# A graph-attention layer on one core: ScalarE fetches a tile in every 32nd pair, its rows between the copy and the exponentials, and SyncE stores before it loads

## The chip, the core and the metric

The kernel runs on one NeuronCore of a Trainium2 chip. Its engines work beside one another, each with its own queue of instructions: TensorE (PE, with its weight loads as PEld), VectorE (DVE), ScalarE (ACT), GpSimd (POOL) and SyncE (SP, which issues DMAs). Each engine takes its queue in order and waits at semaphores for the others. DMAs are issued from SP's, ACT's and POOL's queues. The metric is the time of one execution on the device in microseconds (us), the median over runs.

## The reference

The kernel computes one block of a graph network on 12,500 nodes of 128 features and 400,000 edges sorted by destination; self loops are added. Cut to what matters:

```python
h   = relu(layernorm(x))
hn  = ln(h, ln1_g, ln1_b)
x_l = hn @ W_l                 # for the source of an edge
x_r = hn @ W_r                 # for its destination
m     = leaky_relu(x_l[src] + x_r[dst] + edge_attr @ W_e, 0.2)   # 8 heads of 16
alpha = einsum('ehc,hc->eh', m, att)
a     = softmax of alpha over the edges of one destination, per head
g     = segment_sum(x_l[src] * a, dst) + bias
h2  = h + g
out = x + h2 + gelu(ln(h2, ln2_g, ln2_b) @ W1 + b1) @ W2 + b2
```

The self loops' edge attribute is the mean over all edges, so this mean has to be computed too. The sources of the edges are random, so `x_l[src]` is a gather of 400,000 rows of 528 bytes (128 features and 8 ones) from a table in device memory, `xl_dram`.

## The kernel before

**Start.** A first loop of 43 rounds normalises all nodes, computes `x_l` and stores it to `xl_dram` with four node tiles to a round. In the same rounds POOL gathers some raw rows of `x` (L339), DVE prepares the edge indices, and in round 14 the source indices are loaded: once as the table `src_sb` (128 edges down the partitions, one column to a tile), and once more, number by number, into `hand_sb`, one row of 128 indices for each tile that is fetched by hand (L840 to L847). In round 16 DVE multiplies these by the length of a row in bytes (L851).

**Edges.** 128 edges make a tile, four tiles a pair (of two units of 256 edges), and there are 782 pairs. The main loop (L1681) runs over rounds; in each round every stage works on another pair. In the order of their issue within a round, with the pair that a stage has in hand in round r:

- `gather` (r+4): four indirect gathers from POOL, one for each tile (L1078), into one of 12 row buffers `xs`.
- `own_heads` (r-7): DVE takes each head's own sums from `acc` into the record `rec` (L1215, L1221).
- `keep_turned` (r-5): ACT copies the turned weights from PSUM (L1197).
- `combine` (r): PE turns the gathered rows into `z` (L1143) and adds the destination's and edge's terms with a matmul (L1146).
- `apart` (r-2), `turn` (r-4), `collect` (r-6), `score` (r-2): PE's marking of foreign edges (L1152), transposition of the exponentials (L1192), weighted sums (L1206) and scores (L1167).
- `lowest` (r-3): DVE takes the lowest score (L1173). `slope` (r-1): ACT scales `z` (L1157). `bend` (r-1): DVE's leaky ReLU (L1162). `weigh` (r-3): ACT's two exponentials `p` (L1184). `place` (r+1): DVE marks destinations (L1129).

The order of the work is written out by hand in these tables; no planner moves it. Behind the stages of a round stand, in this order: the loads and sums for the mean edge attribute (`sum_load`, L1248, on SP's queue, every second round up to round 194), the steps of the node groups, the hand-fetched rows, a clearing of states every fourth round, the loads of the next windows every fourth round (`windows`, L1104 to L1119), and the store of one pair's record (`put`, L1230).

**Rows fetched by hand.** Some tiles are not gathered by POOL. In every 22nd pair from 30 on (35 pairs), SP fetches the last tile's 128 rows with one small DMA each; in every 64th pair from 77 on (11 pairs), ACT does. `hand` (L1037 to L1062) spreads the 128 rows over as many rounds as there are pairs in a step: about six rows to a round on SP, two on ACT. Before every 16 rows the queue reads 16 offsets from `hand_sb` into registers (L1010, seen as `TENSOR_LOAD`). The last row is issued seven rounds before its pair's round, and one round before it the queue waits until all rows have landed (L1043). Another 29 pairs read rows that were computed late (`late_dram`) and need no gather.

**Node groups.** Once all edges of some four node tiles are stored as states, a group's steps merge them with the self loop and run the rest of the layer (tables `steps`, and for the last two groups `soon`, `after` and `last_steps`, L1573 to L1657). A state load (`f_state`, L1292) waits for the stores of records. A store of a record waits for earlier accesses to the states unless it is declared free of them; that is done while SP still fetches rows (the list `fetched` is not empty). The second-last group has round 774, the last one 790.

Of the kernel before, what the change touches and what calls it, by code (L numbers as in the profile page):

```python
# [13 lines left out]
F32 = mybir.dt.float32  # L14
# [8 lines left out]
P = 128  # L23
# [52 lines left out]
BESIDE_EVERY = 64  # L76
BESIDE_FIRST = 77
BESIDE_LANDED = 3
BESIDE_AT = 64
BIG = 2.0**126  # L80
# [94 lines left out]
def tile_gnn(  # L175
# [112 lines left out]
    def load_consts():  # L288
        for i, v in enumerate((ln2_g, ln2_b, None, b1[0:P], b1[P : 2 * P])):
            if v is not None:  # L290
                nc.sync.dma_start(cols[:, 2 + i : 3 + i], column(v))
        nc.sync.dma_start(att_c, bass.AP(tensor=att.tensor, offset=att.offset, ap=[[1, C], [C, H], [1, 1]]))
        nc.sync.dma_start(we_sb, bass.AP(tensor=w_e.tensor, offset=w_e.offset, ap=[[P, DE], [0, QP], [1, P]]))
        nc.sync.dma_start(weh_sb[WN:P, :], w_e)
        nc.sync.dma_start(w1_sb, w1)
        nc.sync.dma_start(w2_sb, w2.rearrange("(k p) f -> p k f", p=P))
        nc.sync.dma_start(bias_r, row_bcast(bias, P))
        nc.sync.dma_start(b2_r, row_bcast(b2, P))
        nc.sync.dma_start(first_sb, bass.AP(tensor=dst.tensor, offset=dst.offset, ap=[[0, 1], [UP * U, NU // UP]]))
        for i in range(QP):  # L300
            nc.sync.dma_start(
                at_sb[:, BEHIND:, 1 + i],
                bass.AP(tensor=dst.tensor, offset=dst.offset + (UP * i + 1) * U, ap=[[0, 1], [QU * U, NQU]]),
            )

# [504 lines left out]
    with tc.manual_schedule():  # L810
# [15 lines left out]
        for r in range(max(max(len(qs), 9) + LAST + 1, 16 + PARTS, rows_at[-1] + KEPT + 1)):  # L826
# [11 lines left out]
            if r == 14:  # L838
                nc.sync.dma_start(src_sb, src)
                for at, h in ((0, hands), (BESIDE_AT, beside)):  # L840
                    nc.sync.dma_start(
                        hand_sb[at : at + len(h)],
                        bass.AP(
                            tensor=src.tensor, offset=src.offset + (h[0] + 1) * UP * KU - 1,
                            ap=[[h.step * UP * KU, len(h)], [NCH * K, P]],
                        ),
                    )  # L847
            if r == 16:
                for at, h in ((0, hands), (BESIDE_AT, beside)):
                    rows = hand_sb[at : at + len(h)]  # L850
                    nc.vector.tensor_scalar(rows, rows, float(XW * 4), None, op0=OP.mult)  # L851
# [101 lines left out]
def window_edges(  # L953
# [30 lines left out]
    with ExitStack() as es:  # L984
# [52 lines left out]
        def hand(r, w):  # L1037

            w["new"].clear()
            hands, n = w["pairs"], w["sems"]  # L1040
            i, k = divmod(r + HAND_LEAD + hands.step - hands[0], hands.step)
            if k == HAND_LEAD - 1 and 0 < i <= len(hands):
                all_here = w["queue"].wait_ge(w["landed"][(i - 1) % n], ((i - 1) // n + 1) * P * 16)  # L1043
                tc.declare_fence(all_here.ins, group=f"{w['name']}{i - 1}")
# [3 lines left out]
            if k == 0:  # L1048
                d["x"] = once.tile([P, XW], F32, name=f"{w['name']}{i % 2}")
            for e in range(P * k // hands.step, P * (k + 1) // hands.step):  # L1050
                if e % HAND_READ == 0:
                    d["at"] = words(
                        hand_sb[w["at"] + i : w["at"] + i + 1, e : min(e + HAND_READ, P)], (NT * P - 1) * XW * 4,
                        w["engine"],
                    )
                row = w["queue"].dma_start(
                    d["x"][e : e + 1, :].bitcast(U8), rows_at(xl_dram, d["at"][e % HAND_READ], 1, XW * 4)
                )
# [166 lines left out]
        def put(c):  # L1225
# [11 lines left out]
            if fetched:  # L1237
# [3 lines left out]
                )  # L1241

# [3 lines left out]
        def sum_load(i):  # L1246
            sums[i] = fin.tile([P, LW], F32, name="ea_s", tag="big", bufs=3)
            nc.sync.dma_start(  # L1248
# [295 lines left out]
        def f_put(d):  # L1544
# [4 lines left out]
            (LATE + 1, own_heads),  # L1549
            (5, keep_turned),  # L1550
# [6 lines left out]
            (1, slope),  # L1557
# [3 lines left out]
        )  # L1561
        late_stages = (
            (-WAHEAD, windows),
            (LATE + PUT, put),
# [115 lines left out]
        with tc.manual_schedule():  # L1680
            for r in range(-AHEAD, max(last_round, groups[-1]["round"] + 18)):  # L1681
                in_round(r, early, groups[:-2])
                for late, f in stages:
                    c = r - late
                    if 0 <= c < n_pr:
                        f(c)
                for late, f in sum_stages:
# [11 lines left out]
                for w in ways:  # L1699
                    hand(r, w)  # L1700
# [6 lines left out]
                for late, f in late_stages:  # L1707
                    c = r - late
                    if 0 <= c < n_pr:
                        f(c)  # L1710
# [354 lines left out]
```

## Time and profile before

| | |
|---|---|
| median of 3 runs | 3905.68 us (3905.53 to 3908.12) |
| profiled execution | 3904.92 us |
| its span, first to last instruction | 3903.2 us |
| busy: PE, PEld | 3414.5 us, 2329.9 us |
| busy: DVE, ACT, POOL | 2799.8 us, 2177.5 us, 2913.6 us |
| granted TensorE clock | 0.96 of full speed |

Times in the profile are in us from the span's start, unless marked ns. A row of a group of instructions names the line, the engine, the operation, what is written and read, and how often, and then its busy time, the mean of one in ns, and the idle time of the engine just before such instructions with what ended it. Issuing a DMA, reading registers and waiting at semaphores aren't counted as busy; rows marked SPq, ACTq and POOLq show such work on an engine's queue. A row of the waits gives who waited for whom, the total in us, how often, and the longest. A row of the timeline gives the start, the duration and, in square brackets, the idle time ahead of it. "Issue" in the chain or in the waits is time in which the engine waited for nothing that the profile shows. The name behind an arrow is inferred, and of several semaphores the last one is named.

### The profile page before, as it was taken

To read this page: it belongs to the slowest core of one execution; us is meant where nothing else is said; L and a number is where in the kernel's file an instruction comes from. 1 tells how busy PE (TensorE), PEld (TensorE's weight loads), DVE (VectorE), ACT (ScalarE), POOL (GpSimd) and SP (SyncE) were. 2 spreads that over 40 slices of the span, in tenths; PEclk is the share of its full clock that TensorE was granted. 3 is DMA by queue.
4 is the path that set the end of the run, shared out by engine and by line. 5 is a ranking of instruction groups with operands and counts; after the bars stand their busy time and mean duration, and the time that the engine had idled before them with its cause. 6 is when DMAs were issued, how large, how long until landed. Compare 5 with 4: busy or idle time off the path is not lost.

```text
span 3903.2 us, 70516 instructions
## 1 busy us (share of the span) xinstructions
PE 3414.5 (87%) x18461; PEld 2329.9 (60%) x18463; DVE 2799.8 (72%) x6142; ACT 2177.5 (56%) x4745; POOL 2913.6 (75%) x3092
## 2 busy tenths in 40 slices
PE   3588899889899989998999899999998989898988
PEld 3356566556566666665666666666666666666655
DVE  5577877777776776777777777777777767667665
ACT  6545555555565555555555555655555556456444
POOL 7777777777777777777777777777777777777773
PEclk6799999999999999999999999999999999999999
DMA  8767777777766666665565555555565555555553
GB/s 203 236 163 173 184 184 182 177 185 185 177 135 134 136 131 130 137 132 125 123 131 124 123 126 126 125 123 121 121 125 126 123 123 112 124 122 117 122 119 65
DMA packets 546765, 549.30 MB, mean 141 GB/s; under 512 B 248891, under 2 KB 425372, under 8 KB 545932
## 3 DMA queue, kind: packets, MB, share of 16 engines
q1 hardware_dynamic: 444290, 329.68, 34.3%
q0 software_dynamic: 98528, 214.12, 28.9%
q8 instruction: 150, 2.46, 0.3%
q14 instruction: 261, 2.14, 0.2%
q10 hardware_dynamic: 3536, 0.91, 0.1%
HBM read 482.08 MB, written 62.28 MB: 139 GB/s over the span
## 4 chain that ended last, share of the span: by engine, by line
PE 36%; POOL 24%; DMA 20%; issue 13%; DVE 2%; SPq 1%; ACT 0%; ACTq 0%; POOLq 0%
POOL xs L1078 24%; DMA xs<-xl_dram,src_sb 19%; PE z L1146 8%; PE acc L1206 8%; PE ab L1167 6%; PE pt_ps L1192 4%; PE z L1143 4%; PE ab L1152 2%; PE acc L1525 1%; DMA state<-rec 0%; DVE rec L1173 0%; PE acc L1500 0%; PE pt_ps L759 0%; DMA zw<-xr_dram 0%; PE acc L1328 0%
## 5 line engine op out<-in xcount | busy, mean ns | idle before, releaser
L1078 POOL DMA_INDIRECT xs<-xl_dram,src_sb x2963 | 2798.4, 944 | 904.3 <-issue 783.9
L1184 ACT ACTIVATE p<-ab,rec 128x256 f32<-128x256 f32 x1563 | 656.4, 471 | 923.6 <-DVE rec L1173 909.3
L1215 DVE TENSOR_TENSOR own<-acc,diag 128x272 f32<-128x272 f32 x782 | 342.6, 438 | 821.9 <-PE acc L1206 813.2
L1143 PE MATMUL z<-ident,xs 128*128 128x128 f32 x3079 | 564.7, 283 | 360.6 <-DMA xs<-xl_dram,src_sb 337.9
L1206 PE MATMUL acc<-xs,pt 128*128 128x136 f32 x6158 | 873.7, 286 | 0.0
L1143 PEld LDWEIGHTS z<-ident,xs 128*128 128x128 f32 x3079 | 395.3, 142 | 776.8 <-DMA xs<-xl_dram,src_sb 449.7
L1146 PE MATMUL z<-ea,zw 128*128 128x512 f32 x1564 | 828.0, 612 | 6.5 <-DMA xs<-xl_dram,src_sb 6.5
L1197 ACT COPY pt<-pt_ps 128x512 f32<-128x512 f32 x782 | 456.2, 583 | 643.6 <-PE pt_ps L1192 585.5
L1167 PE MATMUL ab<-m,negrep 128*128 128x512 f32 x1564 | 806.4, 597 | 0.2 <-issue 0.2
L1206 PEld LDWEIGHTS acc<-xs,pt 128*128 128x128 f32 x6158 | 800.7, 197 | 0.0
L1192 PEld LDWEIGHTS pt_ps<-ident,p 128*128 128x128 f32 x3125 | 408.0, 146 | 345.0 <-issue 269.7
L1162 DVE TENSOR_TENSOR m<-z,zs 128x512 f32<-128x512 f32 x782 | 533.6, 682 | 108.1 <-ACT zs L1157 106.2
L1129 DVE TENSOR_SCALAR ea<-dl,wid 96x516 f32<-96x516 bf16 x782 | 575.4, 736 | 8.0 <-DMA dl<-dc_dram 8.0
L1173 DVE TENSOR_REDUCE rec<-ab 128x2 f32<-128x512 f32 x781 | 539.0, 690 | 14.2 <-PE ab L1167 13.7
L1192 PE MATMUL pt_ps<-ident,p 128*128 128x128 f32 x3125 | 490.7, 281 | 0.6 <-ACT p L1184 0.6
L1157 ACT ACTIVATE zs<-z 128x512 f32<-128x512 f32 x782 | 471.8, 603 | 31.0 <-PE z L1146 31.0
L1221 DVE TENSOR_REDUCE rec<-own 128x34 f32<-128x272 f32 x782 | 340.9, 436 | 26.7
L1152 PE MATMUL ab<-ne,farw 128*128 128x512 bf16 (+1 forms) x781 | 306.8, 393 | 24.6 <-ACT p L1184 22.9
L1146 PEld LDWEIGHTS z<-ea,zw 128*128 128x128 f32 x1564 | 253.1, 202 | 7.3 <-issue 6.8
L1167 PEld LDWEIGHTS ab<-m,negrep 128*128 128x128 f32 x1564 | 245.8, 195 | 1.1 <-DMA ea_s<-in_ea_t 0.7
L1152 PEld LDWEIGHTS <-farw 128*128 128x128 bf16 x782 | 78.1, 100 | 211.9 <-issue 102.2
L1184 ACT ACT_TABLE_LOAD x102 | 130.9, 1283 | 1.8
(249 smaller groups left out, 2215.6 us busy)
## 6 DMA issues: line engine op xcount, KB each, us to landing
dl<-dc_dram SPq DMA_DIRECT2D x196, 396.0 KB
hand<-xl_dram SPq DMA_DIRECT2D x4480, 0.5 KB
ea<-in_ea_t SPq DMA_DIRECT2D x196, 256.0 KB
ea_s<-in_ea_t SPq DMA_DIRECT2D x98, 512.0 KB
xs<-xl_dram,src_sb POOLq DMA_INDIRECT x2963
beside<-xl_dram ACTq DMA_DIRECT2D x1408, 0.5 KB
state<-empty SPq DMA_DIRECT2D x98, 144.0 KB
f_st<-state SPq DMA_DIRECT2D x46, 288.0 KB
```

What stands on the lines that cost most here:

```text
L1078: nc.gpsimd.indirect_dma_start(out=xs[:, j, :], out_offset=None, in_=xl_dram, in_offset=bass.IndirectOffsetOnAxis(ap=src_sb[:, c * KP + j ...
L1129: nc.vector.tensor_scalar(d["ea"][0:WN].rearrange("p (a b) -> p a b", b=OW), d["dl"][0:WN].rearrange("p (a b) -> p a b", b=OS)[:, :, 0:OW] ...
L1143: nc.tensor.matmul(z[:, j * P : (j + 1) * P], row_of(c, j)[:, 0:P], ident, start=(j == 0), stop=False, is_transpose=True)
L1146: nc.tensor.matmul(z[:, :e], d["zw"], d["ea"][:, :e], start=False, stop=True)
L1152: nc.tensor.matmul(d["ab"][:, :e], d["far"], d["ne"][:, :e], start=True, stop=False)
L1157: nc.scalar.activation(d["zs"][:, :e], d["z"][:, :e], AF.Copy, scale=SLOPE)
L1162: nc.vector.tensor_tensor(d["m"][:, :e], d["z"][:, :e], d["zs"][:, :e], op=OP.max)
L1167: nc.tensor.matmul(d["ab"][:, :e], negrep.rearrange("p n h -> p (n h)"), d["m"][:, :e], start=False, stop=True)
L1173: nc.vector.tensor_reduce(d["rec"][:, :, CX], d["ab"].rearrange("p (u e) -> p u e", e=U), AX.X, OP.min)
L1184: nc.scalar.activation(d["p"][:, us], d["ab"][:, us], AF.Exp, bias=d["rec"][:, i, CX:SH], scale=-1.0)
L1192: nc.tensor.transpose(d["pt_ps"][:, js], d["p"][:, js], ident)
L1206: nc.tensor.matmul(d["acc"][:, i, :], d["pt"][:, j * P : (j + 1) * P], row_of(c, j), start=(j == js[0]), stop=(j == js[-1]),)
```

## The change

1. ACT fetches a tile in every 32nd pair from 45 on (23 pairs) and not in every 64th from 77 on (11). It issues four rows to a round, all between its copy (`keep_turned`) and its exponentials (`weigh`). `slope` goes ahead of the copy.
2. The hand-fetched indices aren't loaded a second time from device memory. In rounds 24 to 26 of the start, DVE copies their columns out of `src_sb` as floats, PE transposes them, and DVE multiplies and writes `hand_sb`.
3. SP issues the first half of a round's rows at the beginning of the round and the second half behind the node groups' steps; then come the store of a record, the loads of windows and the clearing, in this order. The loads for the mean edge attribute are issued by ACT. The registers of the next four stores are read behind a store.
4. The stores of the records of pairs 779 to 781 are declared free of other accesses to the states too, behind a wait for SP's last fetched rows.
5. The second-last node group's steps are drawn together: exponential, sums, output, statistics, root and scaling lie 1 to 5 rounds behind its state load, not 2 to 8.

```diff
-BESIDE_EVERY = 64
-BESIDE_FIRST = 77
+BESIDE_EVERY = 32
+BESIDE_FIRST = 45
+HAND_ROUND = 24
...
+    def hand_columns():
+        nc.vector.memset(hand_f, 0.0)
+        for at, h in ((0, hands), (BESIDE_AT, beside)):
+            first = (h[0] + 1) * UP * KU - 1
+            step = h.step * UP * KU
+            nc.vector.tensor_copy(
+                hand_f[:, at : at + len(h)], src_sb[:, first : first + step * (len(h) - 1) + 1 : step]
+            )
+    def hand_turn():
+        hand_ps["t"] = once_ps.tile([P, GN * P], F32, name="w_ps")
+        nc.tensor.transpose(hand_ps["t"][0 : BESIDE_AT + len(beside), 0:P], hand_f, ident)
+    def hand_bytes():
+        nc.vector.tensor_scalar(
+            hand_sb, hand_ps["t"][0 : BESIDE_AT + len(beside), 0:P], float(XW * 4), None, op0=OP.mult
+        )
...
-                for at, h in ((0, hands), (BESIDE_AT, beside)):
-                    nc.sync.dma_start(
-                        hand_sb[at : at + len(h)],
...
-        def hand(r, w):
+        def hand(r, w, share=(0, 1), behind=0):
...
-            for e in range(P * k // hands.step, P * (k + 1) // hands.step):
+            first, last = P * k // hands.step, P * (k + 1) // hands.step
+            for e in range(*(first + int((last - first) * x) for x in share)):
...
+            free = bool(fetched) or c > hands[-1]
+            if free and not fetched:
+                nc.sync.wait_ge(ways[0]["landed"][(len(hands) - 1) % LANDED], ((len(hands) - 1) // LANDED + 1) * P * 16)
             store = nc.sync.dma_start(states_at(d["put"])[:, 0:nu], d["rec"][0 : KN * H, 0:nu].bitcast(U8))
-            if fetched:
+            if free:
...
+            if c % QP == 0 and c + QP < n_pr:
+                ats(c // QP + BEHIND + 1)
...
-            nc.sync.dma_start(
+            nc.scalar.dma_start(
                 sums[i],
...
             (LATE + 1, own_heads),
+            (1, slope),
             (5, keep_turned),
...
-            (1, slope),
             (1, bend),
...
+        beside_at = {keep_turned: ()}
         late_stages = (
+            (LATE + PUT, put),
             (-WAHEAD, windows),
-            (LATE + PUT, put),
         )
...
-            (2, f_exp),
-            (3, f_den),
-            (4, f_out),
-            (5, f_h),
-            (6, f_stats),
-            (7, f_root),
-            (8, f_scale),
-            (8, f_rest),
+            (1, f_exp),
+            (2, f_den),
+            (2, f_out),
+            (3, f_h),
+            (3, f_stats),
+            (4, f_root),
+            (5, f_scale),
+            (5, f_rest),
...
+                hand(r, ways[0], (0, 0.5))
...
                         f(c)
+                    if f in beside_at:
+                        hand(r, ways[1], *beside_at[f])
...
-                for w in ways:
-                    hand(r, w)
+                hand(r, ways[0], (0.5, 1))
+                for late, f in late_stages:
...
                 t, off = divmod(r, CLEAR)
...
-                for late, f in late_stages:
```

More of the change, by code (lines that the diff above doesn't have):

```diff
@@ L839, in tile_gnn @@
                 nc.sync.dma_start(src_sb, src)
-                for at, h in ((0, hands), (BESIDE_AT, beside)):
-                    nc.sync.dma_start(
-                        hand_sb[at : at + len(h)],
[L843 to L851, printed above, removed]
+            if r == HAND_ROUND:
+                hand_columns()
+            if r == HAND_ROUND + 1:
+                hand_turn()
+            if r == HAND_ROUND + 2:
+                hand_bytes()
             if r == 10:
```

22 lines of the change are left out of this document (13 added, 9 removed).

## The prediction

> **What bounds the kernel now.** I read the page first, then the waits, the loop in stretches of time, and last the chain of its end.
>
> ```profile
> span 3903.2 us, 70516 instructions
> ...
> PE 3414.5 (87%) x18461; PEld 2329.9 (60%) x18463; DVE 2799.8 (72%) x6142; ACT 2177.5 (56%) x4745; POOL 2913.6 (75%) x3092
> ...
> L1078 POOL DMA_INDIRECT xs<-xl_dram,src_sb x2963 | 2798.4, 944 | 904.3 <-issue 783.9
> ```
>
> By busy share PE leads with 87% and POOL has 75%. The last row corrects that: POOL's 2963 gathers are 2798.4 us busy and 904.3 us idle, 3702.7 us together, which is nearly the whole loop, and the idle time is put down to "issue". The waits say the same:
>
> ```profile
> POOL xs L1078 <- issue: 783.9, 2568, 1.1
> ...
> PE z L1143 <- DMA xs<-xl_dram,src_sb: 337.9, 338, 12.7
> ...
> POOL xs L1078 <- DMA xs<-xl_dram,src_sb: 41.5, 136, 0.3
> ```
>
> (total us, times, longest.) The gap ahead of a gather is 783.9 / 2568 = 0.31 us, and where a releaser is named it is no longer than that (0.3). So POOL never stands still for a buffer: the 0.3 us belongs to each gather. PE, on the other side, waits for gathered rows. The same from the gathers themselves (min/median/max ns, first and last start), and from the gathers' line in three stretches of the loop (length, POOL busy with count):
>
> ```profile
> L1078 POOL DMA_INDIRECT xs<-xl_dram,src_sb x2963: 940/944/1372, 153.9 to 3854.7; - x198
> ```
> ```profile
> 500.00:1000.00 500.00, 378.01 (x401) 0.98 0.77 181
> ...
> 2500.00:3000.00 500.00, 377.94 (x401) 0.98 0.60 124
> 3000.00:3500.00 500.00, 377.99 (x401) 0.96 0.58 121
> ```
>
> (3854.7 - 153.9) / 2962 = 1.249 us per gather, and 401 in every 500 us, whether the DMA engines moved 181 or 121 GB/s. The loop runs at POOL's rate. Could PE follow a faster one? Two pairs after another, late in the kernel, when the rows are there:
>
> ```profile
> 3809.40 0.60 PE L1143 MATMUL z<-ident,xs 128*128 128x128 f32 x4
> ...
> 3813.14 0.60 PE L1143 MATMUL z<-ident,xs 128*128 128x128 f32 x4
> ```
>
> A pair costs PE 3.74 us when it waits for nothing. POOL needs 4 x 1.249 = 5.00 us for a full pair; over all 782 pairs it is 3700.8 / 782 = 4.73 us. PE has about 1 us per pair in hand.
>
> **The change, part by part.** *Gathers.* With a first pair of 45 and a step of 32, ScalarE fetches a tile in 23 pairs instead of 11 (45 + 32 x 22 = 749; 77 + 64 x 10 = 717). So 12 indirect gathers leave POOL: 12 x 1.249 = 15.0 us off the engine that sets the rate. This lies on the path in full unless another engine takes over.
>
> *What ScalarE pays.*
>
> ```profile
> L1056 ACTq DMA_DIRECT2D beside<-xl_dram x1408: 227/228/684, 197.8 to 3521.1; - x176
> ```
> ```profile
> L1010 ACTq TENSOR_LOAD <-hand_sb x88: 1188/1199/1785, 196.5 to 3488.8; - x88
> ```
> ```profile
> 2042.52 0.23 ACTq L1056 DMA_DIRECT2D beside<-xl_dram  x1
> ...
> 2042.84 0.23 ACTq L1056 DMA_DIRECT2D beside<-xl_dram  x1
> ```
>
> A row takes ACT's queue 0.32 us from start to start (2042.52 to 2042.84), and 16 offsets are read in 1.20 us. 1408 rows become 23 x 128 = 2944, 88 reads become 184: 1536 x 0.32 + 96 x 1.20 = 607 us more, or 0.79 us in each of the 23 x 32 = 736 rounds that fetch. A round then has four rows (1.28 us) and in every fourth round a read too (2.48 us). They move from behind the exponentials to between the copy of the turned weights and the exponentials, so queued behind them are the exponentials p, and for p waits PE's turn, a round later. What covers them:
>
> ```profile
> ACT p L1184 <- DVE rec L1173: 909.3, 612, 5.9
> ...
> ACT pt L1197 <- PE pt_ps L1192: 585.5, 464, 7.4
> ```
> ```profile
> 3807.82 0.59 ACT L1197 COPY pt<-pt_ps 128x512 f32<-128x512 f32 x1 [1.00 <-PE pt_ps L1192]
> ...
> 3810.33 0.84 ACT L1184 ACTIVATE p<-ab,rec 128x256 f32<-128x256 f32 x2 [1.43 <-DVE rec L1173]
> ```
>
> ACT idles (909.3 + 585.5) / 782 = 1.91 us per pair ahead of these two. Even in the fast stretch, 2.51 us pass from the copy's start to the exponentials' start, with PE at its own 3.74 us. 1.28 us fits, 2.48 us just fits. I cost it at nothing; if the cover were gone, 0.79 us x 736 = 581 us is the ceiling. The wait for the fetched rows comes five rounds after the last of them was issued, as now. The slope goes ahead of the copy: its z is ready before PE's turn of the same round, so nothing waits longer and the bend on DVE is fed earlier. That is off the path: 0.
>
> *Loads for the edge mean* move from SP's queue to ACT's:
>
> ```profile
> L1248 SPq DMA_DIRECT2D ea_s<-in_ea_t x98: 366/442/1352, 163.1 to 1063.4; - x98
> ```
>
> 0.44 us in every second round, 0.22 us per pair until 1063 us: together with 0.79 us still under the 1.91 us of idle time. 0.
>
> *SP's order.* SP issues half of its rows early in a round, then stores states, then loads windows, then clears. The counts stay. A window's loads now stand behind one store's wait, and SP behind that. Who would notice is DVE's placing and the stored states' reader:
>
> ```profile
> DVE ea L1129 <- DMA dl<-dc_dram: 8.0, 3, 5.7
> ```
>
> DVE waited three times for such a load in the whole run. Windows are loaded four rounds ahead (some 19 us), and the store ahead of them needs a result of the round before. 0, with an end of +2 us (three such waits with POOL's lead of pairs in between).
>
> *Indices.* Two DMAs of single numbers and two multiplications go; a memset, two copies, one PE transposition and one multiplication come, eight to ten rounds later.
>
> ```profile
> 91.15 0.22 DVE L851 TENSOR_SCALAR hand_sb<-hand_sb 35x128 int32<-35x128 int32 x1 [9.73 <-DMA hand_sb<-in_src]
> 92.93 0.37 DVE L851 TENSOR_SCALAR hand_sb<-hand_sb 11x128 int32<-11x128 int32 x1 [1.56 <-DMA hand_sb<-in_src]
> ```
> ```profile
> 151.88 0.94 POOL raw L339
> 152.82 0.06 issue
> ...
> 153.92 0.94 POOL xs L1078
> ```
>
> DVE's stops of 9.73 and 1.56 us go, but POOL is on the chain there, back to back until 152.82. What can be won is the 0.8 us by which its gap of 1.10 us exceeds 0.30; what can be lost is some 2 us, if DVE stops for the index table at the new place. I take 0.
>
> *The second-last node group* does its steps after the state load in rounds 1 to 5 instead of 1 to 8, and the last three pairs' state stores no longer wait for one another. Chain of the end:
>
> ```profile
> 3864.52 1.28 ACT L1449
> 3865.80 0.01 issue
> 3865.81 0.20 ACT f_rstd L1449
> ...
> 3866.69 1.28 ACT L1184
> ...
> 3875.60 1.48 DMA state<-rec
> ...
> 3877.21 1.48 DMA state<-rec
> ...
> 3878.81 1.40 DMA state<-rec
> ...
> 3880.23 2.86 DMA f_st<-state
> ```
> ```profile
> 3868.87 0.22 PE L1152 MATMUL ab<-ne,farw 128*128 128x128 bf16 x1 [1.49 <-ACT p L1184]
> ...
> 3871.25 0.80 PE L1192 MATMUL pt_ps<-ident,p 128*128 128x128 f32 x4 [0.56 <-ACT p L1184]
> ...
> 3876.14 0.30 DVE L1221 TENSOR_REDUCE rec<-own 128x17 f32<-128x136 f32 x1
> ```
>
> The square root's two table loads (1.28 us each) and the normalising stand between the last exponentials, and PE waits 1.49 + 0.56 = 2.05 us for those. Three rounds earlier they lie under POOL's pace. That is -2.05 us; the ends are 0 and the two loads with the root, 2.76 us. In the Trainium skill, "ScalarE: Activation LUTs", section "What ACT_TABLE_LOAD costs", a switch of tables is 1283 ns of load and about 1380 ns of drain; by that, two switches would be worth an estimated 5.3 us and the sum below 2.8 us lower still. The trace agrees with the load and not with the drain: the root starts 0.01 us after it.
>
> The last record is ready at 3876.44, yet its store starts to land at 3878.81, behind two stores of 1.6 us each: 2.37 us, less 0.13 us of issue, is -2.2 us. The ends are 0 and 3.2 us. After that nothing changes: f_st at the end follows as before. The price is DVE: exponential sums, output and statistics now fall in rounds 776 and 777, where PE still waits for rows.
>
> Sum: -15.0 - 2.05 - 2.2 = -19.3 us. The profiled execution took 3904.92 us, 1.7 us more than its span: 3885.7 us. The runs' median is 0.76 us higher, so 3886 us.
>
> **The rivals.** *Only the gathers count:* the crowded DVE rounds 776 and 777 push PE back as far as ACT's freed time brings it forward, and the last stores were not late for the load behind them. Against it: PE has a pair of three gathers and 1.26 us per full pair to catch up. -15.0 us: 3890.7 us.
>
> *PE is the bound:* at 87% it has the highest busy share, so fewer gathers only lengthen POOL's gaps. For it: the share. Against it: 3.74 us per pair against POOL's 4.73 us, and 338 waits for rows. 0 to -4 us: about 3905 us. The Trainium skill says in "Perfetto Trace Analysis", section "Identifying the Most-Contended Engine", that the engine of highest occupancy is the one to optimise first, but it excepts TensorE, for which it takes the share of the weight loads. By that share, 60%, PE stands behind POOL's 75%, and the trace agrees.
>
> *ScalarE becomes the bound (slower):* its own time per pair is 2177.5 / 782 = 2.78 us of busy time, and with four rows and a quarter read, 1.28 + 0.30, it is 4.36 us against POOL's new (3700.8 - 15.0) / 782 = 4.71 us. It decides from 0.35 us per pair of idle time that ACT can't use because it still waits for PE or DVE (it has 1.91 us now). At 0.45 us the fetching rounds cost 736 x 0.10 = 74 us more: 3960 us. Against it: the rows of the trace show queue issues running while an activation runs, and POOL's twelve row buffers let PE lag by several pairs.
>
> **How the numbers follow.** Forecast (3882 to 3889 us) 0.66; only the gathers 0.20; PE the bound 0.06; ScalarE the bound 0.08. The range takes in the first two with the ends of the unknown terms: below, -15.0 - 0.8 - 2.76 - 3.2 = -21.8 us, 3884 against the median, and 3 us for what three earlier rounds may bring besides, so 3881; above, -15.0 + 2 + 2 = -11 us, 3894.7 us, so 3895. It leaves out 0.14. A measurement here can tell about 0.2%, 7.8 us, from no change: the first two cases are faster, the third the same, the fourth slower.
>
> **What would show it.** Right: 2951 gathers still 1.249 us apart, the last some 15 us earlier; 23 tiles by ScalarE; p waiting less for rec, by about what the rows take; no PE wait for p after the last gather, and the last three state stores side by side. Wrong: POOL waits longer than 0.3 us (a buffer held back, so PE or ACT sets the rate), a first loop gather clearly off 153.9, or a longer stretch than 47.6 us from the last gather's end (3855.6) to the end.

## The result and the profile after

| | before | after |
|---|---|---|
| median | 3905.66 us (3902.41 to 3908.12, 12 runs) | 3895.44 us (3887.48 to 3903.11, 12 runs) |
| profiled execution, its span | 3904.92 us, 3903.2 us | 3898.61 us, 3896.8 us |

The ratio is 0.9974 with a 95% interval of 0.9967 to 0.9982. The change makes the kernel 10.2 us faster, where the prediction's sum was 19.3 us; the median lies 0.4 us above the range. The profiled execution of after is 3.2 us above its median, so its trace shows 6.4 us of gain in the span.

The page of after: the span, the engines' busy time, and the row of the gathers (busy us, mean ns of one, idle us ahead of them).

```profile
span 3896.8 us, 74415 instructions
...
PE 3418.9 (88%) x18462; PEld 2345.5 (60%) x18464; DVE 2793.9 (72%) x6144; ACT 2151.3 (55%) x4745; POOL 2901.9 (74%) x3080
...
L1097 POOL DMA_INDIRECT xs<-xl_dram,src_sb x2951 | 2787.3, 945 | 914.2 <-issue 749.2
```

Twelve gathers are gone as predicted (2951 for 2963), and one takes what it took. (A row that they gather is 136 numbers of four bytes, by the code: 544 bytes, not 528.) But the idle time ahead of the gathers has grown. Before it was 904.3 / 2963 = 0.305 us for each, and by that 2951 gathers should have 900.6 us. They have 914.2, so 13.6 us of POOL's time were lost in waits that weren't there. The gathers' own row (min/median/max ns, first and last start), and POOL's work on them in stretches of 500 us, say where:

```profile
L1097 POOL DMA_INDIRECT xs<-xl_dram,src_sb x2951: 938/944/1086, 152.0 to 3852.3; - x197
```
```profile
500.00:1000.00 500.00, 372.97 (x396) 0.95 0.70 177
1000.00:1500.00 500.00, 372.32 (x395) 0.95 0.60 141
1500.00:2000.00 500.00, 378.03 (x401) 0.97 0.58 134
```

Five or six gathers are missing in each of the first two stretches, and none later. In the first stretch before had 401. The loop is as long as before (3852.3 - 152.0 = 3700.3 us against 3700.8), although it has 15.0 us less to gather. The start is 1.9 us shorter (152.0 against 153.9). From the end of the last gather to the end of the span it is 3896.8 - 3853.2 = 43.6 us against 47.6, 4.0 us shorter. So -1.9 - 15.0 + 13.6 - 4.0 is -7.3 us, where the span shows -6.4. Of the 0.9 us between them 0.8 is counted twice: the first gather's own gap, 1.10 us before and 0.30 after, is part of the shorter start and of the gathers' idle time.

Two of POOL's stops in the timeline of after (idle time and releaser in the brackets; it is 0.3 ahead of most gathers):

```profile
1094.01 0.94 POOL L1097 DMA_INDIRECT xs<-xl_dram,src_sb  x1 [2.27 <-PE acc L1225]
...
1118.23 0.94 POOL L1097 DMA_INDIRECT xs<-xl_dram,src_sb  x1 [5.81 <-PE acc L1225]
```

POOL waits for the weighted sums that free a row buffer, so PE is late by more than the twelve buffers cover. Why is PE late? First the waits of after (us in total, times, longest), on the engines and on SP's queue, and then the one row of before's SP queue that answers to it:

```profile
DVE ea L1148 <- DMA dl<-dc_dram: 63.2, 17, 8.2
...
PE z L1162 <- SPq L1060: 38.5, 9, 7.4
...
POOL xs L1097 <- PE acc L1225: 36.1, 74, 5.8
```
```profile
SPq L1252 <- DMA state<-empty: 181.5, 83, 4.5
```
```profile
SPq L1230 <- DMA state<-empty: 5.4, 10, 1.0
```

SP's store of a record waited for the landing of a clear 10 times and 5.4 us in all before; now 83 times and 181.5 us. Behind that store SP has its fetched rows, the wait for all of a tile's rows (L1060), and the windows. PE waits for L1060 for 38.5 us (4.8 before), and DVE for a window's `dl` for 63.2 us (8.0 before). The chain of after shows one such clear down to PE, and 27 us later a window's load that lands late (start, us, what; pieces between are left out where "..." stands):

```profile
1025.99 6.51 DMA state<-empty
1032.50 0.02 SPq L1252
...
1035.51 0.02 SPq L1060
...
1035.57 0.47 PE z L1162
...
1062.51 7.04 DMA dl<-dc_dram
1069.58 0.76 DVE ea L1148
...
1070.52 1.10 PE z L1165 x2
```

And SP's queue at the same place:

```profile
1023.83 0.34 SPq L1123 DMA_DIRECT2D ea<-in_ea_t  x1
1024.22 0.43 SPq L1128 DMA_DIRECT2D dl<-dc_dram  x1
1024.70 0.61 SPq L1133 DMA_DIRECT2D du<-du_dram  x1
1025.45 0.49 SPq L1138 DMA_DIRECT2D zw<-xr_dram  x1
1025.99 0.61 SPq L809 DMA_DIRECT2D state<-empty  x1
1026.71 2.24 SPq L1075 DMA_DIRECT2D hand<-xl_dram  x6
1032.62 0.36 SPq L1252 DMA_DIRECT2D state<-rec  x1
```

The clear, 144 KB, is issued right behind four loads of 256, 396, 64 and 48 KB and lands 6.5 us after its issue. The next store can't be issued before, at 1032.62, and SP stands still from 1028.95 on (1026.71 + 2.24). The rows behind it are late, and PE with them.

### The profile page after: what moved, and what is told of

Same layout as the page of the kernel before. It is cut to its first block, busy times and chain, and to the rows that moved or that the text cites. A ratio compares the mean times of both kernels' runs of the same rounds, so it can differ in the third digit from the quotient of the medians.

```text
span 3896.8 us, 74415 instructions
## 1 busy us (share of the span) xinstructions
PE 3418.9 (88%) x18462; PEld 2345.5 (60%) x18464; DVE 2793.9 (72%) x6144; ACT 2151.3 (55%) x4745; POOL 2901.9 (74%) x3080
## 4 chain that ended last, share of the span: by engine, by line
PE 43%; DMA 20%; POOL 17%; issue 10%; DVE 5%; SPq 3%; ACT 2%; ACTq 0%; POOLq 0%; DVEq 0%
POOL xs L1097 16%; DMA xs<-xl_dram,src_sb 15%; PE z L1165 10%; PE acc L1225 10%; PE ab L1186 8%; PE pt_ps L1211 5%; PE z L1162 5%; PE ab L1171 3%; DMA dl<-dc_dram 1%; DVE rec L1192 1%; DMA zw<-xr_dram 1%; PE acc L1549 1%; DVE ea L1148 1%; DMA du<-du_dram 1%; ACT h_sb L613 1%
## 5 line engine op out<-in xcount | busy, mean ns | idle before, releaser
L1097 POOL DMA_INDIRECT xs<-xl_dram,src_sb x2951 | 2787.3, 945 | 914.2 <-issue 749.2
L1203 ACT ACTIVATE p<-ab,rec 128x256 f32<-128x256 f32 x1563 | 655.9, 471 | 1246.3 <-DVE rec L1192 1149.8
L1165 PE MATMUL z<-ea,zw 128*128 128x512 f32 x1564 | 843.5, 622 | 26.9 <-DMA zw<-xr_dram 17.2
L1162 PE MATMUL z<-ident,xs 128*128 128x128 f32 x3067 | 534.7, 282 | 284.7 <-DMA xs<-xl_dram,src_sb 232.4
L1148 DVE TENSOR_SCALAR ea<-dl,wid 96x516 f32<-96x516 bf16 x782 | 575.7, 736 | 63.2 <-DMA dl<-dc_dram 63.2
L1192 DVE TENSOR_REDUCE rec<-ab 128x2 f32<-128x512 f32 x781 | 538.2, 689 | 14.6 <-PE ab L1186 14.3
L1216 ACT COPY pt<-pt_ps 128x512 f32<-128x512 f32 x782 | 459.1, 587 | 38.2 <-PE pt_ps L1211 36.9
L1165 PEld LDWEIGHTS z<-ea,zw 128*128 128x128 f32 x1564 | 253.6, 203 | 31.5 <-DVE ea L1148 25.3
```

Source lines behind the costliest of these rows:

```text
L1097: nc.gpsimd.indirect_dma_start(out=xs[:, j, :], out_offset=None, in_=xl_dram, in_offset=bass.IndirectOffsetOnAxis(ap=src_sb[:, c * KP + j ...
L1148: nc.vector.tensor_scalar(d["ea"][0:WN].rearrange("p (a b) -> p a b", b=OW), d["dl"][0:WN].rearrange("p (a b) -> p a b", b=OS)[:, :, 0:OW] ...
L1162: nc.tensor.matmul(z[:, j * P : (j + 1) * P], row_of(c, j)[:, 0:P], ident, start=(j == 0), stop=False, is_transpose=True)
L1165: nc.tensor.matmul(z[:, :e], d["zw"], d["ea"][:, :e], start=False, stop=True)
L1192: nc.vector.tensor_reduce(d["rec"][:, :, CX], d["ab"].rearrange("p (u e) -> p u e", e=U), AX.X, OP.min)
L1203: nc.scalar.activation(d["p"][:, us], d["ab"][:, us], AF.Exp, bias=d["rec"][:, i, CX:SH], scale=-1.0)
```

## The experiments

Theory 1, from these rows: the clear in last place, behind the windows' loads, is what loses the 13.6 us; everything else of the change does what was predicted. Theory 2: the loads for the mean edge attribute on ACT's queue delay PE. Theory 3: the doubled rows on ACT, ahead of the exponentials, delay PE. Some kernels (e4, e6, both e10, and e11 to e18) ran on chips on which the kernel before takes 4946 to 5020 us; they are told at the end of this section, and each is compared only with the kernel before on its own chip.

**SP's end of a round as before (e1).** In the changed kernel, the clear is issued ahead of the windows' loads and the store behind them.

```diff
         late_stages = (
-            (LATE + PUT, put),
             (-WAHEAD, windows),
+            (LATE + PUT, put),
         )
...
                 hand(r, ways[0], (0.5, 1))
-                for late, f in late_stages:
-                    c = r - late
-                    if 0 <= c < n_pr:
-                        f(c)
                 t, off = divmod(r, CLEAR)
...
+                for late, f in late_stages:
+                    c = r - late
+                    if 0 <= c < n_pr:
+                        f(c)
```

> The changed kernel with SP's end of a round as before: clear, then loads of windows, then the store of a record. Theory 1 (the clear stands behind the windows' loads, lands late, and the next round's store waits for it, so that SP, then PE, then POOL fall behind): the stores wait for clears under 20 us in all instead of 181.5 us, POOL's stops for a row buffer fall from 14 us to under 2 us, and the time falls by about 13 us to 3882 us. Theory 2 (the 512 KB loads on ScalarE's queue hold up the windows' loads): the stops stay near 14 us and the time near 3895 us. Theory 3 (the doubled rows on ScalarE hold up the exponentials and so PE): the same as theory 2, 3895 us.

Measured: 3883.75 us (3882.39 to 3885.34) against 3906.1 for before, ratio 0.9944 (0.9931 to 0.9958). The rows that answer to those of after, from the page, the gathers, and SP's and DVE's waits:

```profile
span 3881.9 us, 74432 instructions
...
L1097 POOL DMA_INDIRECT xs<-xl_dram,src_sb x2951 | 2787.5, 945 | 900.1 <-issue 749.6
```
```profile
L1097 POOL DMA_INDIRECT xs<-xl_dram,src_sb x2951: 940/944/1688, 152.2 to 3838.5; - x197
```
```profile
SPq L1252 <- DMA state<-empty: 35.4, 40, 2.3
```
```profile
DVE ea L1148 <- DMA dl<-dc_dram: 11.8, 4, 7.7
```

The idle time is 900.1 us where 900.6 were due: no stop is left. SP's waits for a clear are 35.4 us, where I had expected under 20. The last gather starts 13.8 us earlier than in after, and the loop is 3686.3 us, 14.5 less than before's. The order of three groups of DMAs on one queue was worth 3895.44 - 3883.75 = 11.7 us, 0.30% by the two ratios (0.9974 and 0.9944, each with before of its own chip).

A clear ahead of the loads takes its time too (start, us, what). Two of them in the chain of e1, each with SP's store behind it:

```profile
705.54 4.38 DMA state<-empty
...
1109.98 3.89 DMA state<-empty
```

In after the chain has 6.51 us (above) and 4.05 us (from 1157.33 on). So two things differ: how late the clear lands, and what SP issues before it needs the landing. In e1 that is four loads (1110.49 to 1113.44), in after six rows, 2.2 us.

**Store, then clear, then windows (e2).** Only the clear goes ahead of the loads; the store stays ahead of both.

```diff
-                for late, f in late_stages:
+                for late, f in late_stages[:1]:
...
                 t, off = divmod(r, CLEAR)
...
+                for late, f in late_stages[1:]:
+                    c = r - late
+                    if 0 <= c < n_pr:
+                        f(c)
```

> The changed kernel with the store first, then the clear, then the loads of windows. Theory 1: the clear lands ahead of the windows' bytes, a round before the next store; the stores' waits for clears fall under 40 us, POOL's stops under 2 us, time about 3882 us. If it is not the clear but that windows stand behind a store's wait: the stops stay at 14 us and the time near 3895 us. Theories 2 and 3: 3895 us.

Measured: 3885.48 us (3884.06 to 3886.64), ratio 0.9948 (0.9934 to 0.9961).

```profile
L1097 POOL DMA_INDIRECT xs<-xl_dram,src_sb x2951 | 2787.0, 944 | 900.6 <-issue 749.8
```

Again 900.6 us, no stop. So it is the clear's place behind the loads that costs, not the store's place ahead of them. Here the loads and a round's rows lie between a clear and the next store (1020.69 to 1027.63 in one round), and SP no longer waits for a clear at all but for one wait of 0.2 us. How much of the cost is the later landing and how much is the little work that is left to cover it, no run separates.

**The edge-mean loads back on SP (e3).**

```diff
-            nc.scalar.dma_start(
+            nc.sync.dma_start(
                 sums[i],
```

> The changed kernel with the 98 loads for the edge mean issued by SP again. Theory 1: the stores' waits for clears stay over 120 us, some stops of POOL stay, time 3888 to 3897 us. Theory 2: landing of the windows' loads goes back to some 5 us, POOL's stops go, about 3882 us. Theory 3: 3895 us.

Measured: 3923.85 us (3919.39 to 3927.06), ratio 1.0043 (1.0029 to 1.0057).

```profile
L1097 POOL DMA_INDIRECT xs<-xl_dram,src_sb x2951 | 2786.7, 944 | 939.7 <-issue 753.8
```
```profile
SPq L1252 <- DMA state<-empty: 211.8, 90, 4.4
```

Theory 2 falls, and with the other sign: with the 512 KB loads on SP's queue POOL loses 939.7 - 900.6 = 39.1 us. Their move to ACT, costed at nothing, saves some 25 us of POOL's time as long as the clear is last. The time lies 27 us above what theory 1 expected at most. What I hadn't counted is that DVE waits for these loads themselves, 88.5 us here and 0.9 us in before. How much of the 39.1 us that makes isn't shown.

**The doubled rows alone (e5).** The kernel before with 23 pairs on ACT, nothing else.

```diff
-BESIDE_EVERY = 64
-BESIDE_FIRST = 77
+BESIDE_EVERY = 32
+BESIDE_FIRST = 45
```

> The kernel before with nothing changed but the 23 pairs in place of 11 (four rows to a round on ScalarE, behind the exponentials). Theories 1 and 2: 2951 gathers 1.249 us apart without a stop, so 15.0 us less than before, 3890.7 us. Theory 3: POOL stops by several us between 800 and 1130 us and the gain is under 10 us, over 3895 us.

Measured: 3906.54 us (3903.39 to 3907.72), ratio 1.0000 (0.9991 to 1.0009).

```profile
L1078 POOL DMA_INDIRECT xs<-xl_dram,src_sb x2951: 940/944/1792, 170.6 to 3857.1; - x197
```
```profile
109.71 0.22 DVE L851 TENSOR_SCALAR hand_sb<-hand_sb 23x128 int32<-23x128 int32 x1 [18.23 <-DMA hand_sb<-in_src]
```
```profile
111.55 0.94 POOL L339 DMA_INDIRECT raw<-in_x,lead  x1 [14.47 <-DVE roots_sb L622]
```

The loop takes 3857.1 - 170.6 = 3686.5 us, the same as in e1. So the rows cost the loop nothing at their old place behind the exponentials, and e1 has them at the new place without a stop: theory 3 falls. But the loop begins 16.6 us later and the whole gain is gone: DVE stops 18.23 us for the 23 rows of single indices, where it stopped 1.56 us for 11, and POOL's raw gathers stand behind DVE. I had expected 3890.7 us in all. Without the indices turned on the chip, the doubled rows would have brought nothing.

**The change without its rows and without its order (e20).** As e1, with 11 pairs on ACT (every 64th from 77).

> The changed kernel with SP's old order and only 11 pairs fetched by ScalarE, so the change without its rows and without its order. On a chip whose kernel before runs in 3906 us, POOL's gathers set the rate: 12 gathers, 15.0 us, more than SP's old order with 23 pairs (3883.75), so 3898.7 us, and the tail 4 us shorter than before. On a chip whose kernel before runs in about 5000 us there are two theories: if the rows on ScalarE cost there, more than SP's old order with 23 pairs gained there (0.4 to 0.5% with the tail's parts undone), 0.98 to 0.985 of before, below the 0.9892 that 11 pairs gave with the clear last; if the rows cost nothing there, about 0.995.

Measured, on a chip whose before takes 3904.45 us: 3898.77 us (3897.49 to 3904.99), ratio 0.9987 (0.9977 to 0.9997).

```profile
L1097 POOL DMA_INDIRECT xs<-xl_dram,src_sb x2963: 940/944/1154, 152.5 to 3854.2; - x198
```

Against e1 it is 15.0 us more, which is 12 gathers; by the two ratios, 0.43%, it is 16.8 us. The loop takes 3701.7 us, and what is left of the gain lies at the start and at the end: 1.4 us there (152.5 for 153.9) and 5.5 us here (from 3855.2 to 3897.2).

**The order alone, in the kernel before (e19).** Store, windows, clear; 11 pairs, and the edge-mean loads on SP.

```diff
         late_stages = (
-            (-WAHEAD, windows),
             (LATE + PUT, put),
+            (-WAHEAD, windows),
         )
...
+                for late, f in late_stages:
+                    c = r - late
+                    if 0 <= c < n_pr:
+                        f(c)
                 t, off = divmod(r, CLEAR)
...
-                for late, f in late_stages:
-                    c = r - late
-                    if 0 <= c < n_pr:
-                        f(c)
```

> The kernel before, with only SP's order at the end of a round changed to the new one: store, windows, clear last; 11 pairs fetched by ScalarE. On a chip whose kernel before runs in 3906 us, theory 1 expects 20 to 40 us of stops of POOL, 3925 to 3945 us; the rival, that the order costs only together with the doubled rows, 3903 to 3909 us. On a chip whose kernel before runs in about 5000 us: 0.5 to 0.8% above before, as the same order cost on such chips so far.

Measured, on e20's chip: 4005.78 us (4002.0 to 4009.59), ratio 1.0256 (1.0239 to 1.0273).

```profile
L1078 POOL DMA_INDIRECT xs<-xl_dram,src_sb x2963 | 2798.0, 944 | 1009.1 <-issue 781.0
```
```profile
SPq L1230 <- DMA state<-empty: 248.9, 91, 4.8
```
```profile
DVE ea L1129 <- DMA dl<-dc_dram: 120.5, 47, 6.5
...
PE z L1143 <- SPq L1043: 80.4, 15, 9.9
```

The order costs by itself, in the direction of theory 1, but 2.5 to 5 times what I had expected (20 to 40 us): POOL loses 1009.1 - 904.3 = 104.8 us, and all of the 101 us are there. So the change's other parts soften its own order, from 105 to 14 us. Taking the edge-mean loads off SP is one of them (39 to 14 in e3). In e19 too DVE waits for these loads, 89.8 us. What brings it from 105 to 39, the split of SP's rows, the registers read ahead, or anything else, no run separates.

**The parts of the tail (e11, e12, e17, e18).** Each is e1 with one part of the change undone: the second-last group's steps in their old rounds (e11, e17), and the last stores not free (e12, e18).

```diff
-            (1, f_exp),
-            (2, f_den),
-            (2, f_out),
-            (3, f_h),
-            (3, f_stats),
-            (4, f_root),
-            (5, f_scale),
-            (5, f_rest),
+            (2, f_exp),
+            (3, f_den),
+            (4, f_out),
+            (5, f_h),
+            (6, f_stats),
+            (7, f_root),
+            (8, f_scale),
+            (8, f_rest),
```
```diff
-            free = bool(fetched) or c > hands[-1]
+            free = bool(fetched)
```

> The changed kernel with SP's old order, and the second-last group's eight closing steps at the old rounds (2 to 8 in place of 1 to 5). The loop is the same, so the last loop gather ends as with the old order alone. Prediction's size of this term: the stretch from the last gather's end to the end of the span grows by 2.05 us, 3885.8 us. Rival (the last three stores' freedom alone carried the tail): the stretch as before within 0.5 us, 3883.75.

> The changed kernel with SP's old order, and the stores of the sums behind the last fetched pair no longer released from the fence of the fetched rows (free as before the change). Prediction's size of this term: the stretch from the last gather's end to the end grows by 2.2 us, 3885.95 us. Rival (the closing steps alone carried the tail): the stretch as before within 0.5 us, 3883.75.

> The changed kernel with SP's old order, and the second-last group's eight closing steps at their old rounds (2 to 8 in place of 1 to 5). On a chip whose kernel before runs in 3906 us. Prediction's size: the stretch from the end of the last gather to the end of the span grows from the 42.5 us of SP's old order by 2.05 us to 44.5, 3885.8 us. Rival (this term carried nothing): 42.5 within 0.5, 3883.75.

> The changed kernel with SP's old order, and the stores of the sums behind the last fetched pair not released from the fence of the fetched rows, as before the change. On a chip whose kernel before runs in 3906 us. Prediction's size: the stretch from the end of the last gather to the end of the span grows from 42.5 us by 2.2 us to 44.7, 3885.95 us. Rival (this term carried nothing): 42.5 within 0.5, 3883.75.

Measured: e11 0.9964 (0.9944 to 0.9984) and e12 0.9954 (0.9935 to 0.9974) of before's 5019.69 us; e17 0.9965 (0.9943 to 0.9986) and e18 0.9949 (0.9926 to 0.9971) of 4946.41 us. On these chips neither differs from the other, and the times decide nothing. The end of a trace still does, for one part. From the last record's reduction on DVE to the last state load's issue on SP, in after, e17 (stores free) and e18 (not free):

```profile
3871.67 0.30 DVE L1240 TENSOR_REDUCE rec<-own 128x17 f32<-128x136 f32 x1
```
```profile
3873.64 0.94 SPq L1316 DMA_DIRECT2D f_st<-state  x2
```
```profile
4902.48 0.30 DVE L1240 TENSOR_REDUCE rec<-own 128x17 f32<-128x136 f32 x1
```
```profile
4904.77 0.94 SPq L1316 DMA_DIRECT2D f_st<-state  x2
```
```profile
4889.95 0.30 DVE L1240 TENSOR_REDUCE rec<-own 128x17 f32<-128x136 f32 x1
```
```profile
4894.31 0.94 SPq L1316 DMA_DIRECT2D f_st<-state  x2
```

Where the stores are free it is 1.97 us in after and 2.29 in e17; where they aren't, 4.36 us in e18, and 3880.23 - 3876.14 = 4.09 us in before by the prediction's rows. e11 (free) and e12 (not free) repeat it with 2.28 and 4.28 us. The freedom is worth some 2.1 us.

The steps show in these four traces too (e11, e12, e17, e18), and there they don't pay. From the eleventh-last record's reduction to the last it is 27.48 us with the old steps (e11, e17) and 24.46 and 23.61 with the new (e12, e18). But for the three records ahead of these it is 16.3 and 16.1 us with the old steps and 23.2 and 21.7 with the new: in these traces the time only moves to earlier rounds. On chips like that of before no run undoes the steps alone. There, from the last gather's end to the last record, it is 18.4 us in after, 17.1 in e1, and 18.9, 19.0 and 16.9 in e2, e3 and e20; with the old steps it is 20.5 in before, 19.2 in e5 and 21.2 in e19.

**Chips on which POOL doesn't set the rate (e4, e6, e10, e13 to e16).** e4 is the changed kernel with 11 pairs on ACT; e6, e13 and e15 are the kernel of e19; both e10, e14 and e16 are e1 with a step of 24 (31 pairs; e14 and e16 too) or 16 (47 pairs).

```diff
-BESIDE_EVERY = 32
-BESIDE_FIRST = 45
+BESIDE_EVERY = 24
+BESIDE_FIRST = 37
```

> The changed kernel with 11 pairs fetched by ScalarE in place of 23, all else as changed. Theory 1 (the clear behind the windows' loads): the stores still wait some 180 us for clears, POOL still stops for 8 to 14 us between 800 and 1130 us, and 12 gathers come back: about 3908 us. Theory 3 (ScalarE's doubled rows are part of the lag): the stops are gone, 2963 gathers at 1.249 us with the shorter start and end: 3905.7 - 1.9 - 4.0 = 3900 us.

> The kernel before with only SP's end of a round changed: store, windows, clear. Theory 1: the stores wait for clears as long as in the run with the sums on SP (some 200 us in place of 5.4), POOL stops some 30 to 40 us, all before 1200 us, and the time is 3935 to 3945 us, slower than before. If the order hurts only together with the change's other parts: 3905 us.

> The changed kernel with SP's old order (as in e1) and a tile fetched by ScalarE in every 24th pair from 37 on: 31 pairs, eight gathers less than with 32. If POOL still sets the rate: 8 x 1.249 = 10.0 us less than e1's 3883.8 us, 3873.8 us, without stops. If ScalarE (the prediction's slower rival: 2.78 us of busy time a pair and 5.33 rows at 0.32 us with a third of a read, 4.89 us against 4.70 us of POOL) becomes the bound: POOL stops and the time is 3890 us or more.

> As the run before with every 16th pair from 29 on: 46 or 47 pairs, 23 or 24 gathers less than with 32. If POOL still sets the rate: about 29 us less than e1, 3855 us. If ScalarE becomes the bound (2.78 + 8 x 0.32 + 0.6 = 5.94 us a pair against 4.68 us if nothing overlaps): POOL stops all along, up to some 900 us slower, or in part if the issues overlap with activations: over 3900 us.

> The kernel before, with only SP's order at the end of a round changed to the new one: the store of the sums, the windows' loads, and the clear last. 11 pairs are fetched by ScalarE, the edge-mean loads stay on SP. Theory 1 (the clear's landing behind the windows' loads holds the next store and with it SP): POOL's stops come in this kernel too, some 20 to 40 us of them as in the changed kernel with the edge-mean loads back on SP (39.4), so 3925 to 3945 us. Rival (the order costs only together with ScalarE's doubled rows): within 3 us of before's 3905.7 and no stop of a gather in the loop above 0.45 us.

> The changed kernel with SP's old order, and ScalarE fetching a tile in every 24th pair from pair 37 (31 pairs, 8 more). If POOL's gathers still set the rate: 8 x 1.249 = 10.0 us less than the 3883.75 of every 32nd, so 3873.8, with the last loop gather 10 us earlier. Rival (ScalarE's row issues begin to bound the pairs): the last loop gather not earlier by more than 5 us, stops of POOL above 0.45 us released by PE or ScalarE, 3879 us or more.

> The kernel before, with only SP's order at the end of a round changed to the new one: the store of the sums, the windows' loads, and the clear last; 11 pairs fetched by ScalarE, the edge-mean loads on SP. On a chip whose kernel before runs in 3906 us. Theory 1 (the clear's landing behind the windows' loads holds the next store and with it SP): POOL's stops come here too, 20 to 40 us of them, so 3925 to 3945 us. Rival (the order costs only together with ScalarE's doubled rows): within 3 us of 3905.7 and no stop of a gather in the loop above 0.45 us.

> The changed kernel with SP's old order and 31 pairs fetched by ScalarE (every 24th from pair 37). On a chip whose kernel before runs in 3906 us. If POOL's gathers set the rate: 8 x 1.249 = 10.0 us below the 3883.75 of every 32nd pair, 3873.8. Rival (ScalarE's row issues bound the pairs): the last loop gather not earlier by more than 5 us, 3879 us or more.

Measured, as ratios to before on the same chip: e4 0.9892 (0.9859 to 0.9924); the order alone 1.0050 (1.0028 to 1.0071), 1.0080 (1.0052 to 1.0107) and 1.0084 (1.0060 to 1.0108); 31 pairs 0.9983 (0.9959 to 1.0007), 0.9981 (0.9961 to 1.0001) and 0.9993 (0.9973 to 1.0013); 47 pairs 0.9964 (0.9945 to 0.9983). What such a chip looks like, in the page and the waits of e4:

```profile
span 4951.2 us, 71271 instructions
...
L1097 POOL DMA_INDIRECT xs<-xl_dram,src_sb x2963 | 2796.6, 944 | 1908.1 <-issue 759.6
```
```profile
PEld z L1162 <- issue: 487.1, 842, 21.0
...
POOL xs L1097 <- PE acc L1225: 453.7, 130, 13.4
...
ACT p L1203 <- issue: 241.7, 125, 8.6
```

A gather takes 944 ns as ever, but POOL has 1908 us of idle time, of which 454 us are waits for PE's sums, and in the chain that ended last POOL has 1% and PE 37%. So POOL doesn't set the rate there. That PE's own work does isn't shown either: at a granted clock of 0.892 a pair that waits for nothing still takes it 3.73 us (`z` begins at 2000.72 and 2004.45 in e4). What is longer are the stops: some 140 times more than 8 us pass from one pair's L1165 to the next, some 1520 us together, where before has 7 such times. Some are waits for SP's late rows (140.0 us of PE's waits for L1060), and PE's weight loads stand for 487 us ahead of `z` alone without a wait that the profile shows. Why they stand isn't shown. The order alone costs on these chips as well, 0.5 to 0.8%. The expected gain of 10 us from 31 pairs doesn't come there, nor could it: fewer gathers help only where POOL is the bound. The row issues on ACT do come to stand ahead of the exponentials: the time there that is put down to no other engine is 241.7 us here with 11 pairs, and with 47 pairs, in the second e10,

```profile
ACT p L1203 <- issue: 1040.0, 362, 7.9
```

Yet the time doesn't follow the number of pairs (0.9983 with 31, 0.9964 with 47), so that ScalarE's rows are a cost there isn't shown. e4 was the fastest of these, with 11 pairs and the clear last; it differs from the others in both, on one chip, so it doesn't tell which it was. Whether 31 pairs would be faster than 23 on a chip like the first stays open; no run of it fell on one. The fastest version measured is e1: the change with SP's old order, 22.4 us below before and 11.7 below after. e2 isn't clear of it (their intervals overlap).

## Why the prediction was right in direction and wrong in size

*Gathers, -15.0 us:* right. e1's and e5's loops are 14.5 and 14.3 us shorter than before's 3700.8, and e20 against e1 is 15.0 us.

*What ScalarE pays, 0:* right where POOL sets the rate. e5 has the rows at the old place and e1 at the new one, and neither loop has a stop. The sign I had named for it didn't come: `p` waits longer for `rec` and not less (1149.8 us in after, 1118.0 in e1, 909.3 before). Instead the wait of the copy went, from 585.5 to 36.9 us in after. The wait for the fetched rows comes six rounds after the last of them, by the code, not five.

*Loads for the edge mean, 0:* wrong with the order that was measured, where they are worth 25 us (e3) in the change's favour. What they are worth with the clear not last no run shows.

*SP's order, "0, with an end of +2 us":* this is the step that failed. It measured 13.6 us of stops of POOL in the trace, and 11.7 us between the medians of after and e1. I asked what the windows' loads now stand behind (one store's wait), and who waits for those loads. I didn't ask what now stands behind them: the clear. Nor did I ask who waits for the clear's landing. The trace of before had it: SP's store waits for the clear, 10 times and 5.4 us. With the issues of four loads between the clear and the store that wait was short. In the round shown the clear, behind 764 KB of loads, lands 6.5 us after its issue and has only six row issues, 2.2 us, to hide it. The store comes late, behind it SP's rows and the next windows, and PE falls behind POOL until the twelve buffers are used up. The prediction's end of +2 us came from counting the three waits that the trace of before had for a load, under the old order, and a new order doesn't keep that count. Its signal for being wrong, POOL waiting longer than 0.3 us for a buffer, appeared. (So did a first gather off 153.9, but that is the shorter start below.)

*Indices, 0 with ends -0.8 and +2:* the start became 1.9 us shorter, beyond the lower end. The last raw gather and the first of the loop in after:

```profile
150.75 0.94 POOL L361 DMA_INDIRECT raw<-in_x,src_raw  x1 [0.30 <-issue]
152.00 0.94 POOL L1097 DMA_INDIRECT xs<-xl_dram,src_sb  x1 [0.30 <-issue]
```

The gap between them is back from 1.10 to 0.30, and the raw gathers end 1.1 us earlier (150.75 for 151.88). As an accounting of the change this was nearly right. As an account of why it gains it was not: with 23 rows the old way of loading would have cost 16.6 us (e5), and I had costed it by the 11 rows of before.

*The tail, -2.05 and -2.2 us:* right in sum, 4.0 us in after and 5.1 in e1 (there from 3839.4 to 3881.9). The freedom of the stores is shown as 2.1 us (e18 against e17, e12 against e11). The drawn-together steps are only read, as the 2.1 us of after and the 3.4 of e1 between the last gather's end and the last record, and behind the last gather PE has no wait for `p` any more. Other parts of the change are in these figures too, and on the slower chips the rounds ahead took the gain back (e12, e18), as the rival "only the gathers count" had it. From the state load's issue to the end it is as long as before (23.2 in after, 23.0 before).

*The rivals:* PE as the bound falls by e1 on chips like that of before, where fewer gathers brought 14.5 us. ScalarE as the bound doesn't occur on chips like that of before (e1, e5). "Only the gathers count", 3890.7 us, came nearer than the forecast by its number. That is luck: its reason, a tail that gains nothing, didn't hold on this chip (4.0 us).

## What to carry to other kernels

When a group of DMAs moves on a queue, ask of every DMA that ends up behind it who waits for its landing, and what is left between the two to cover it. A wait that the trace shows as rare and short is a dependency that is covered by what stands between; count what stands between after the change. And where a size is doubled, cost every place that scales with it, the preparation too, before crediting the part of the change that replaces it with nothing.

## What the runs showed that I had not expected

A 144 KB store into device memory lands 6.5 us after its issue in one round behind 764 KB of loads on the same queue, and 4.05 us in another; ahead of the loads it took 3.89 and 4.38 us in e1. In the old order the store that waits for it waited at most 1.0 us in before and 2.3 us in e1.

Loading single numbers across rows grew steeply: DVE waited 1.56 us for 11 rows of 128 and 18.23 us for 23, behind the same 35 rows. By these waits that is 1.1 ns and 6.2 ns for each number, so that the smaller load gave no measure for the larger. Why isn't shown.

The same order costs 14 us with the rest of the change around it and 105 us in the kernel before, so a term of this kind can't be added up from parts.
